# A shared feed-forward's second stage in seven products per unit, added onto rows of x1

## Chip, core, metric

The kernel runs on one core of a Trainium2 chip. The metric is the device time of one execution in microseconds. Everything is float32.

## What is computed

```python
# first layer: modulated linear layer, residual
ys = y * scale
d  = rsqrt(einsum('bi,io->bo', ys*ys, weight*weight) + EPS)
x1 = x + einsum('bsi,io->bso', x * ys[:, None, :], weight) * d[:, None, :]

# second layer on 4096 rows of 512: shared feed-forward, and 8 experts of which 2 per row
shared = silu(xf @ w1) * (xf @ w3) @ w2            # 512 -> 1024 -> 512
h      = gelu(einsum('nc,ech->enh', xf, W1e))
y      = einsum('enh,ehc->enc', h, W2e)
routed = einsum('ne,enc->nc', combine, y)          # combine: the gates of the top 2
out    = x1 + (shared + routed) / 3
```

## The kernel before

The 4096 rows of x1 are 8 blocks of 512 (`NB`, `TB`). After a prologue that makes x1 block by block (features on the partitions, in `big`, and rows in the DRAM tensor `x1_d`), a list of units runs, one after the other: the shared feed-forward of blocks 0 to 5 (`early` = 6), 4 units a block (`HU`); then 32 slots, each 256 rows of one expert, and behind a switch as many further slots as the routing needs (2 in this run: 34 in all); then the shared units of blocks 6 and 7. These last two blocks are called the tail here.

**A shared unit** makes 256 of the 1024 hidden columns for 512 rows. Its first stage already is a scheme of seven products in place of eight for a 2 x 2 block product: `product` (L696) with n from 1 to 7, each for w1 and w3, each of two matmuls of 128x128 by 256 columns. One PSUM half, `chain`, gathers products 1, 6, 5 and 3, and ScalarE (`evict`, L741) copies it out between them; `other` holds 2, 4 and 7, and VectorE adds them on (`add`, L746). `begin` issues products 1 and 2, `rest` (L750) the others, the silu, and the product into `h`. The sums of blocks that such a scheme needs are made beforehand on VectorE, `token_sums` for x1 and `weight_sums` for w1 and w3.

**Its second stage** is `second(m)` (L789), plain: for one of the unit's two 128-column pieces of h, four matmuls (one per 128 rows) with all 512 columns of w2. They gather in four PSUM banks over the whole block, `py`. It is issued by the *next* unit's `rest`, in two places (behind product 5 and behind the product into h), so that h is ready. At a block's end L808 adds a third of each bank onto the rows of x1, which `fetch_row` has brought; blocks 0 to 5 store the sum in DRAM as `base_d` (from ScalarE's queue, L810), the tail writes the output (L812).

**A slot** (`Slot`) works the same way, with its second stage in four parts (`part0` to `part3`), issued by the next slot. Its expert's weights, W1e and W2e, take two tiles of `big` (`expert`, L817): slot j takes pair j mod 3. `fetch_first` and `fetch_second` bring them over SP's queue; in the steady state three slots ahead. Its rows are gathered by GpSimd, its result goes to `ys_d` in two stores.

**In the tail** each unit calls `pump` four times, 32 times in all. A pump adds picks (`add_picks`, L1004: for a tile of 128 rows the two experts' rows, times their gates, onto the held row tile) and starts gathers for others (`gather_picks`, L987: fetch the tile's row sum, two indirect transfers from `ys_d` into one of ten places in `big`). Tile i of 32 is gathered in pump 25i/32 rounded down, and added six pumps later.

The order of all engines is written out by hand: each engine runs its instructions as the program issues them. `tasks` (L1046 to L1075) names what else is issued at two points of each unit's `rest`: task 2n and 2n+1 belong to unit n. In a list of tasks, `6 * HU` is task 24, hence unit 12, the first of block 3.

Of the kernel before, what the change touches and what calls it, by code (L numbers as in the profile page):

```python
# [32 lines left out]
P = 128  # L33
# [11 lines left out]
def kernel(  # L45
# [458 lines left out]
    def row_tile(name):  # L504
        return later["row"].tile([P, D], FP, tag="row", name=name)

    def open_pools():
        lin_ctx.close()
        later["row"] = ctx.enter_context(tc.tile_pool(name="row", bufs=15))
        work = ctx.enter_context(tc.tile_pool(name="work", bufs=1))  # L510
        t_tiles.append(work.tile([P, 3 * KH * TH], FP, name="t1"))
        later["g"] = work.tile([P, 2 * TB], FP, name="g")
        later["h"] = [work.tile([P, 2 * TB], FP, name=f"h{i}") for i in range(2)]
        rt = rt_ctx.enter_context(tc.tile_pool(name="rt", bufs=1))
        for name in ("sel", "hit", "one", "two"):
            later[name] = rt.tile([P, NT, E], FP, name=name)
        for name in ("picked", "run"):
            later[name] = rt.tile([P, E, NT], FP, name=name)
        for name in ("top", "den", "live", "half"):
            later[name] = rt.tile([P, NT], FP, name=name)  # L520
        for name in ("cnt", "shift", "ns", "upto"):
            later[name] = rt.tile([P, E], FP, name=name)
        later["last"] = rt.tile([P, E + 1], FP, name="last")
        later["full"] = rt.tile([P, E, N // GS], FP, name="full")
        later["edge"] = rt.tile([P, N // GS], FP, name="edge")
        later["own"] = rt.tile([P, NSLOT, E], FP, name="own")
        later["ownf"] = rt.tile([P, NSLOT], FP, name="ownf")
        later["high"] = [rt.tile([P, NT], I32, name=f"high{i}") for i in range(2)]
        later["low"] = [rt.tile([P, NT], I32, name=f"low{i}") for i in range(2)]
        later["addr"] = addr  # L530
        later["toks_raw"] = toks_raw
# [138 lines left out]
    def pump():  # L670

        if not passed:
            return
        for work in pumps.get(passed[0], []):
            work()
        passed[0] += 1

    held = {}

    def fetch_row(t, rows_d):  # L680
        held[t] = row_tile(f"row{t}")
        nc.sync.dma_start(out=held[t], in_=rows_d[ts(t, P)])

    class Shared:
# [62 lines left out]
        def rest(self, prev, task):  # L750
            g, h = self.c = [t.rearrange("p (m t) -> p m t", m=2) for t in (later["g"], later["h"][self.at % 2])]
            self.h = h
            self.evict(0, LO)
            for i in range(2):
                self.product(self.chain[i][:, LO], i, 6, False)
                if not self.seven:
                    self.product(self.other[i][:, HI], i, 7, True)
            self.add(LO, 0, LO)
            pump()
            self.evict(1, LO)  # L760
            for i in range(2):
                self.product(self.chain[i][:, LO], i, 5, False)
            self.evict(1, HI)
            if prev is not None:
                prev.second(0)
            self.add(HI, 1, HI)
            pump()
            for i in range(2):
                self.product(self.chain[i][:, LO], i, 3, False)
            nc.scalar.activation(g[:, 0, HI], self.chain[0][:, LO], AF.Silu)  # L770
            nc.scalar.activation(g[:, 0, LO], g[:, 0, LO], AF.Silu)
            nc.vector.tensor_tensor(h[:, 0, HI], g[:, 0, HI], self.chain[1][:, LO], ALU.mult)  # L772
            nc.vector.tensor_tensor(h[:, 0, LO], g[:, 0, LO], h[:, 0, LO], ALU.mult)
            task(2 * self.at)
            pump()
            if prev is not None:
                prev.second(1)
            for i in range(2):
                self.product(self.other[i][:, HI], i, 4, False)
            self.add(HI, 1, LO)  # L780
            nc.scalar.activation(g[:, 1, :], g[:, 1, :], AF.Silu)
            nc.vector.tensor_tensor(h[:, 1, :], g[:, 1, :], h[:, 1, :], ALU.mult)
            task(2 * self.at + 1)
            pump()

        def parts(self):
            return [lambda: self.second(0), lambda: None, lambda: self.second(1), lambda: None]

        def second(self, m):  # L789
# [12 lines left out]
            if blk < early and HSC - 1 > hc >= HSC - 1 - NS:  # L802
                fetch_row(blk * NS + hc - (HSC - 1 - NS), x1_d)
            if hc == HSC - 1:
                for s in range(NS):
                    t = blk * NS + s
                    r = held.pop(t)
                    nc.vector.scalar_tensor_tensor(r, self.py[blk][s], third, r, ALU.mult, ALU.add)  # L808
                    if blk < early:
                        nc.scalar.dma_start(out=base_d[ts(t, P)], in_=r)  # L810
                    else:
                        nc.sync.dma_start(out=out_f[ts(t, P)], in_=r)  # L812
# [4 lines left out]
    def expert(j):  # L817
        weights[j] = (big[j % PAIRS * 2], big[j % PAIRS * 2 + 1])
# [39 lines left out]
    class Slot:  # L858
# [26 lines left out]
        def rest(self, prev, task):  # L885
            parts = prev.parts()
# [61 lines left out]
        def parts(self):  # L948
            return [self.part0, self.part1, self.part2, self.part3]

        def part0(self):
            j = self.j
            self.r = [row_tile(f"yr{j}_{s}") for s in range(SUB)]
# [17 lines left out]
        def part3(self):  # L971
# [5 lines left out]
            for s in range(SUB):  # L977
                nc.scalar.dma_start(out=ys_d[ds(j * GS + s * P, P)], in_=self.r[s])
# [8 lines left out]
    def gather_picks(t):  # L987

        fetch_row(t, base_d if t < early * NS else x1_d)
        spot = len(order) % 10 * 2  # L990
# [13 lines left out]
    def add_picks(t):  # L1004
        for i, y in enumerate(picks.pop(t)):
            nc.vector.scalar_tensor_tensor(held[t], y, gate[i][:, t : t + 1], held[t], ALU.mult, ALU.add)  # L1006
        if t < early * NS:
            nc.sync.dma_start(out=out_f[ts(t, P)], in_=held.pop(t))
# [14 lines left out]

    def turn_last():
        x1T[last_blk] = big[0]
        for k in range(KC):
            nc.vector.transpose(big[0][:, k, :], later["segs"][:, : TB // Q, ts(k, Q)])

# [17 lines left out]
    for u, work in (  # L1046
# [6 lines left out]
        (6 * HU, [lambda: fetch_weights(0)]),  # L1053
# [3 lines left out]
        (8 * HU + 2, [lambda: fetch_weights(1)]),  # L1057
        (10 * HU + 4, [lambda: turn_rows(0)]),
        (2 * early * HU, [lambda: fetch_weights(2)]),
        (2 * late, [reload_last]),  # L1060
# [13 lines left out]
    for blk in range(1, early):  # L1074
        tasks[2 * blk * HU - 3].append(lambda blk=blk: token_sums(blk))  # L1075
    mine = list(range(early * NS))
    mine = [early * NS + i for i in range(NS)] + mine[: len(mine) // 2] + list(range(NT - NS, NT)) + mine[len(mine) // 2 :]
    points = 4 * TAIL * HU
    for i, t in enumerate(mine):
        p = i * (points - 7) // len(mine)  # L1080
        pumps.setdefault(p, []).append(lambda t=t: gather_picks(t))
        pumps.setdefault(p + 6, []).insert(0, lambda t=t: add_picks(t))
# [10 lines left out]
    for u, unit in enumerate(units):  # L1093
        if u == late:
            for n in tc.Switch(later["spare"], E):
# [8 lines left out]
                for part in last.parts():  # L1104
                    part()
# [3 lines left out]
        if u == late:  # L1109
            passed.append(0)  # L1110
            token_sums(early)
# [3 lines left out]
    prev.second(0)  # L1115
    prev.second(1)
# [39 lines left out]
```

## Time and profile before

| | |
|---|---|
| runs shown, us | 1220.57, 1212.42, 1218.62 (median 1218.62) |
| profiled execution | 1208.25 us, span 1206.5 us, mean granted TensorE clock 0.997 |
| busy, share of the span | TensorE 99%, VectorE 46%, ScalarE 19%, GpSimd 37% |
| prologue (to the first unit's second stage) | 0 to about 160 us |
| blocks 0 to 5 | to about 591 us |
| slots | about 591 to 1048 us |
| tail | about 1048 to 1206.5 us |
| shared unit, TensorE | 18.95 us, of which the second stage 6.87 |

PE is TensorE's matmuls, PEld its weight loads, DVE VectorE, ACT ScalarE, POOL GpSimd, SP the engine that issues most transfers. In the tables of groups a row has the line, engine, operation, output and inputs, shape and count; then busy time and the mean duration of one in ns; then how long its engine sat idle before it. In timelines a row begins with its start and the time it covers, both in us. A program's float32 matmul is two records. A matmul's duration includes a stretch in which the next one is already running, so what it costs is the distance to the next one's start. The same holds, less strongly, for VectorE.

### The profile page before, as it was taken

The numbers are of one execution on the slowest core, as the hardware profiler recorded it, in microseconds if no ns is written. First come the engines' busy times: TensorE is split into PE (matmuls) and PEld (weight loads), VectorE is DVE, ScalarE is ACT, GpSimd is POOL, SyncE is SP. The second block draws the span as 40 slices with busy tenths as digits, with TensorE's granted clock in tenths as the row PEclk, the third lists the DMA queues.
The fourth block names the chain that finished last, engine by engine and source line by source line (L and its number), as shares of the span: only waits on it lengthen the run. The fifth ranks groups of instructions, "written<-read, shape, count | busy, mean of one in ns | idle before, by whom it ended". The sixth has DMA issues, their size and how long they took to land.

```text
span 1206.5 us, 14504 instructions
## 1 busy us (share of the span) xinstructions
PE 1189.7 (99%) x4802; PEld 895.5 (74%) x4802; DVE 552.6 (46%) x1264; ACT 225.6 (19%) x515; POOL 449.4 (37%) x448
## 2 busy tenths in 40 slices
PE   9999999999999999999999999999999998999998
PEld 6444666777767677676688888888888887777765
DVE  4546465422323223332255455455455453447664
ACT  2000121211112112121121221221221221121111
POOL 3000000343530112101456676676676670066540
PEclk9999999999999999999999999999999998999999
DMA  9598503201103032110198898999899996287862
GB/s 173 111 230 187 105 27 104 46 0 36 36 1 110 24 133 87 36 70 5 34 253 261 228 236 242 252 238 246 246 238 245 252 241 193 83 258 251 309 227 79
DMA packets 121587, 184.91 MB, mean 153 GB/s; under 512 B 15236, under 2 KB 50180, under 8 KB 121496
## 3 DMA queue, kind: packets, MB, share of 16 engines
q1 hardware_dynamic: 83384, 117.63, 38.0%
q0 software_dynamic: 16448, 35.26, 10.3%
q10 hardware_dynamic: 21664, 30.94, 8.1%
q8 instruction: 40, 0.66, 0.3%
q14 instruction: 51, 0.42, 0.2%
HBM read 139.14 MB, written 44.64 MB: 152 GB/s over the span
## 4 chain that ended last, share of the span: by engine, by line
PE 94%; DMA 4%; DVE 1%; issue 1%; SPq 0%; ACTq 0%; ACT 0%; DVEq 0%
PE ph L875 19%; PE ch L717 18%; PE ps L795 18%; PE ot L717 14%; PE yc L933 9%; PE pl L443 8%; PE yo L933 7%; DMA big<-in_L_cond_W1e_dram 2%; DMA seg<-in_x_dram 1%; PE pq L372 1%; DMA ys_d<-yr 1%; DMA w0t<-in_L_cond_weight_dram 0%; PE pr L388 0%; DVE xT L282 0%; DVE row L1006 0%
## 5 line engine op out<-in xcount | busy, mean ns | idle before, releaser
L844 POOL DMA_INDIRECT xsegs<-x_d,toks x280 | 307.1, 1097 | 327.4 <-issue 127.7
L795 PE MATMUL ps<-w_sb,h 128*128 128x512 f32 x512 | 230.0, 592 | 0.0
L648 POOL DMA_INDIRECT tok_d<-token,addr x64 | 63.5, 992 | 289.7 <-DVE addr L638 275.1
L795 PEld LDWEIGHTS ps<-w_sb,h 128*128 128x128 f32 x512 | 97.3, 190 | 95.6 <-issue 92.1
L875 PE MATMUL ph<-xg,big 128*128 128x256 f32 x544 | 130.3, 383 | 5.0 <-issue 4.3
L946 DVE TENSOR_TENSOR yr<-yo,yr 128x256 f32<-128x256 f32 x102 | 43.3, 424 | 191.0 <-ACT yr L943 95.3
L875 PE MATMUL ph<-t,big 128*128 128x256 f32 x544 | 128.5, 379 | 0.0
L875 PEld LDWEIGHTS ph<-xg,big 128*128 128x128 f32 x544 | 104.3, 192 | 21.0 <-issue 5.6
L443 PE MATMUL pl<-xT,wm 128*128 128x512 f32 (+1 forms) x288 | 117.0, 554 | 0.8 <-DVE big L354 0.4
L748 DVE TENSOR_TENSOR g<-ot,g 128x256 f32<-128x256 f32 x96 | 40.6, 423 | 161.9 <-PE ot L717 139.1
L875 PEld LDWEIGHTS ph<-t,big 128*128 128x128 f32 x544 | 103.4, 190 | 14.1
L717 PE MATMUL ot<-big,w_sb 128*128 128x256 f32 x448 | 110.3, 379 | 0.0
L996 POOL DMA_INDIRECT big<-ys_d,addr x64 | 69.3, 1082 | 101.5 <-PE ch L717 58.6
L717 PEld LDWEIGHTS ot<-big,w_sb 128*128 128x128 f32 x448 | 85.0, 190 | 12.4 <-issue 0.8
L443 PEld LDWEIGHTS pl<-xT,wm 128*128 128x128 f32 x288 | 52.4, 190 | 52.1 <-issue 46.5
L943 ACT ACTIVATE yr<-yc 128x256 f32<-128x256 f32 x136 | 52.3, 384 | 204.7 <-PE yc L933 194.4
L933 PE MATMUL yc<-w0t,g 128*128 128x256 f32 x272 | 69.9, 379 | 0.5 <-ACT yr L943 0.5
L883 ACT ACTIVATE h<-ph 128x512 f32<-128x512 f32 x68 | 40.6, 598 | 157.6 <-PE ph L875 157.6
L748 DVE TENSOR_TENSOR h<-ot,h 128x256 f32<-128x256 f32 x96 | 40.6, 423 | 60.3 <-PE ot L717 48.7
L772 DVE TENSOR_TENSOR h<-g,ch 128x256 f32<-128x256 f32 x32 | 13.5, 421 | 118.1 <-PE ch L717 115.6
L717 PE MATMUL ch<-w0t,seg 128*128 128x256 f32 x256 | 62.6, 380 | 2.5 <-issue 2.5
L717 PE MATMUL ch<-t,seg 128*128 128x256 f32 x256 | 63.1, 379 | 0.0
(184 smaller groups left out, 1454.4 us busy)
## 6 DMA issues: line engine op xcount, KB each, us to landing
big<-in_L_cond_W1e_dram SPq DMA_DIRECT2D x140, 256.0 KB, 6.2
big<-in_L_cond_W2e_dram SPq DMA_DIRECT2D x34, 1024.0 KB, 6.4
ys_d<-yr ACTq DMA_DIRECT2D x68, 256.0 KB, 5.5
x_d<-back SPq DMA_DIRECT2D x32, 256.0 KB, 4.8
row<-x_d SPq DMA_DIRECT2D x32, 256.0 KB, 4.6
out_dram<-row SPq DMA_DIRECT2D x32, 256.0 KB, 4.0
base_d<-row ACTq DMA_DIRECT2D x24, 256.0 KB, 4.2
row<-base_d SPq DMA_DIRECT2D x24, 256.0 KB, 4.9
```

Of the source, the lines that this page charges most:

```text
L443: nc.tensor.matmul(pas[oc][:, ds(lo, n)], lhsT=wms[b][:, k, oc, :], rhs=xTs[blk][:, k, ds(lo, n)], start=(k == 0), stop=(k == KC - 1),)
L648: ins = nc.gpsimd.indirect_dma_start(out=tok_d, out_offset=bass.IndirectOffsetOnAxis(ap=later["addr"][i][:, t : t + 1].bitcast(U32), axis= ...
L717: nc.tensor.matmul(out, lhsT=lhs[:, k, :], rhs=rhs[:, k, :], start=start and k == 0, stop=k == KH - 1, skip_group_check=not start,)
L748: nc.vector.tensor_tensor(c[:, m, cols], p[:, half], c[:, m, cols], ALU.add)
L795: nc.tensor.matmul(self.py[blk][s], lhsT=self.h[:, m, ts(s, P)], rhs=w2_sb[:, hc, :], start=(hc == 0), stop=(hc == HSC - 1),)
L844: nc.gpsimd.indirect_dma_start(out=seg[:, q, :], out_offset=None, in_=x1_segs, in_offset=bass.IndirectOffsetOnAxis(ap=toks[:, c : c + 1].b ...
L875: nc.tensor.matmul(self.ph[:, i], lhsT=weights[j][0][:, k, ts(c, P)], rhs=xg[j][:, k, :], start=(k == 0), stop=(k == KC - 1),)
L883: nc.scalar.activation(self.h[:, ds(c - i, per), :], self.ph, AF.Gelu)
L933: nc.tensor.matmul(out, lhsT=a[:, k, :], rhs=b[:, k, :], start=start and k == 0, stop=k == HC // 2 - 1, skip_group_check=not start,)
L943: nc.scalar.activation(self.r[r][:, cols], self.chain[:, LO], AF.Copy)
L946: nc.vector.tensor_tensor(self.r[r][:, cols], self.other[:, half], self.r[r][:, cols], ALU.add)
L996: nc.gpsimd.indirect_dma_start(out=picks[t][i], out_offset=None, in_=ys_d, in_offset=bass.IndirectOffsetOnAxis(ap=at.bitcast(U32), axis=0) ...
```

## The change

In blocks 1 to 7 the second stage becomes the 7-product scheme, over the unit's 256 hidden columns and 512 rows. h is taken as 2 x 2 blocks (`a11` to `a22`: rows 0 to 255 or 256 to 511, first or second 128 hidden columns), and so is the unit's part of w2. Block 0 keeps the plain form (`plain`).

- `hidden_sums`: 4 VectorE sums at a unit's end make s1, s2, s4 and, in place, a21.
- `out_sums`: 3 VectorE sums per unit of a block, t1, t2 and t4, in block 1 (held in `big[0]`) and once more for the tail (`big[5]`); in block 1 also one in place in w2.
- `seconds(part)`: 14 matmuls of 256 columns in four parts, into three banks: `chain` takes four products, `two` one, `seven` two.
- `drain(part)`: 7 VectorE operations add a third of a bank onto the base rows at once, unit by unit; `chain` is drained after each of its products and filled again. So the block's sums no longer gather in PSUM.
- The base rows are fetched at a block's start, in tiles of two 128-row tiles (`pair_tile`, 6 of them in place of 15 row tiles), and stored by SP. Rows fetched for the tail use GpSimd's segment buffer too. Sums, outputs and `ys_d` also move in pairs.
- The tiles of `big` are dealt to the slots in another way, and weights are fetched at other tasks; picks have eight places in `big[1]` to `big[4]`.
- In the tail, tiles 0 to 19 are picked before block 7's, 20 to 23 after it.

```diff
-    held = {}
-    def fetch_row(t, rows_d):
-        held[t] = row_tile(f"row{t}")
-        nc.sync.dma_start(out=held[t], in_=rows_d[ts(t, P)])
+    def fetch_pairs(blk, tiles=None):
+        base[blk] = tiles or [pair_tile(f"base{blk}_{m}") for m in range(2)]
+        for m, r in enumerate(base[blk]):
+            nc.sync.dma_start(out=r, in_=as_pair(x1_d, blk * TB + m * TH))
+    def out_sums(u, home):
+        tiles = [home.rearrange("p k (n d) -> p (k n) d", d=TH)[:, n] for n in range(8)] + later["more"]
+        t1, t2, t4 = out_map[u] = tiles[3 * u : 3 * u + 3]
+        b1, b2 = w2_sb[:, 2 * u, :], w2_sb[:, 2 * u + 1, :]
+        b11, b12, b21, b22 = b1[:, LO], b1[:, HI], b2[:, LO], b2[:, HI]
+        if u not in summed:
+            nc.vector.tensor_tensor(b12, b22, b12, ALU.subtract)
+            summed.add(u)
+        nc.vector.tensor_tensor(t2, b12, b11, ALU.add)
+        nc.vector.tensor_tensor(t1, b22, t2, ALU.subtract)
+        nc.vector.tensor_tensor(t4, b21, t2, ALU.subtract)
...
             self.evict(1, LO)
+            mm, drain = parts[0]
+            mm()
+            drain()
             for i in range(2):
                 self.product(self.chain[i][:, LO], i, 5, False)
             self.evict(1, HI)
-            if prev is not None:
-                prev.second(0)
+            mm, drain = parts[1]
+            mm()
             self.add(HI, 1, HI)
+            drain()
             pump()
             for i in range(2):
                 self.product(self.chain[i][:, LO], i, 3, False)
...
+            mm, drain = parts[2]
+            mm()
             nc.vector.tensor_tensor(h[:, 0, HI], g[:, 0, HI], self.chain[1][:, LO], ALU.mult)
             nc.vector.tensor_tensor(h[:, 0, LO], g[:, 0, LO], h[:, 0, LO], ALU.mult)
+            drain()
             task(2 * self.at)
             pump()
-            if prev is not None:
-                prev.second(1)
             for i in range(2):
                 self.product(self.other[i][:, HI], i, 4, False)
+            mm, drain = parts[3]
+            mm()
             self.add(HI, 1, LO)
             nc.scalar.activation(g[:, 1, :], g[:, 1, :], AF.Silu)
+            drain()
             nc.vector.tensor_tensor(h[:, 1, :], g[:, 1, :], h[:, 1, :], ALU.mult)
+            if self.blk > 0:
+                self.hidden_sums()
             task(2 * self.at + 1)
             pump()
+        def hidden_sums(self):
+            s1, s2, s4 = later["hs"]
+            nc.vector.tensor_tensor(s1, a21, a22, ALU.add)
+            nc.vector.tensor_tensor(s2, s1, a11, ALU.subtract)
+            nc.vector.tensor_tensor(a21, a11, a21, ALU.subtract)
+            nc.vector.tensor_tensor(s4, a12, s2, ALU.subtract)
+        def seconds(self, part):
...
+            for out, a, b, start in (
+                [(chain, a11, b1[:, LO], True), (two, a12, b2[:, LO], True)],
+                [(seven, a21, b1[:, HI], True), (chain, s2, t2, False)],
+                [(chain, s1, t1, False)],
+                [(chain, s4, b2[:, HI], False), (seven, a22, t4, False)],
+            )[part]:
+                for s in range(2):
+                    nc.tensor.matmul(out[:, s], lhsT=a[:, ts(s, P)], rhs=b, ...)
+        def drain(self, part):
+            for bank, m, half in (
+                [(chain, 0, LO), (two, 0, LO)],
+                [(seven, 1, HI), (chain, 1, LO)],
+                [(chain, 1, HI)],
+                [(chain, 0, HI), (seven, 1, LO)],
+            )[part]:
+                r = base[blk][m][:, :, half]
+                nc.vector.scalar_tensor_tensor(r, bank, third, r, ALU.mult, ALU.add)
+            if part == 3 and self.u == HU - 1:
+                self.store()
...
-        weights[j] = (big[j % PAIRS * 2], big[j % PAIRS * 2 + 1])
+        weights[j] = ((big[2], big[3]), (big[4], big[5]), (big[1], big[0]))[j % PAIRS]
...
-            for s in range(SUB):
-                nc.scalar.dma_start(out=ys_d[ds(j * GS + s * P, P)], in_=self.r[s])
+            nc.scalar.dma_start(out=as_pair(ys_d, j * GS), in_=self.pair)
...
-        spot = len(order) % 10 * 2
+        spot = len(order) % 8 * 2
...
-        (6 * HU, [lambda: fetch_weights(0)]),
+        (8 * HU + 1, [lambda: fetch_weights(0)]),
-        (8 * HU + 2, [lambda: fetch_weights(1)]),
+        (10 * HU + 1, [lambda: fetch_first(1)]),
+        (10 * HU + 4, [lambda: fetch_first(2)]),
         (10 * HU + 4, [lambda: turn_rows(0)]),
-        (2 * early * HU, [lambda: fetch_weights(2)]),
-        (2 * late, [reload_last]),
+        (2 * early * HU, [lambda: fetch_second(1), lambda: fetch_second(2)]),
+        (2 * late, [reload_last, lambda: out_sums(0, big[5])]),
+        (2 * late + 1, [lambda: out_sums(1, big[5])]),
+        (2 * late + 3, [lambda: out_sums(2, big[5])]),
...
+    for blk in range(early):
+        tasks[2 * blk * HU].append(lambda blk=blk: fetch_pairs(blk))
+    for u in range(HU):
+        tasks[2 * HU + 2 * u].append(lambda u=u: out_sums(u, big[0]))
...
-    prev.second(0)
-    prev.second(1)
+    for mm, drain in prev.parts():
+        mm()
+        drain()
```

## The prediction, made blind

> **What bounds the kernel now.** I read the page's busy table first, then the chain of waits, the costliest groups, and last the timelines of the places that the change touches. The page:
>
> ```profile
> PE 1189.7 (99%) x4802; PEld 895.5 (74%) x4802; DVE 552.6 (46%) x1264; ACT 225.6 (19%) x515; POOL 449.4 (37%) x448
> ...
> PE 94%; DMA 4%; DVE 1%; issue 1%; SPq 0%; ACTq 0%; ACT 0%; DVEq 0%
> PE ph L875 19%; PE ch L717 18%; PE ps L795 18%; PE ot L717 14%; PE yc L933 9%; PE pl L443 8%; PE yo L933 7%; DMA big<-in_L_cond_W1e_dram 2%; DMA seg<-in_x_dram 1%; PE pq L372 1%; DMA ys_d<-yr 1%; DMA w0t<-in_L_cond_weight_dram 0%; PE pr L388 0%; DVE xT L282 0%; DVE row L1006 0%
> ...
> L795 PE MATMUL ps<-w_sb,h 128*128 128x512 f32 x512 | 230.0, 592 | 0.0
> ```
>
> TensorE is busy 99% of the span and 94% of the chain. L795, which the change replaces in seven blocks of eight, is 18% of the chain and never waits (idle 0.0). So PE time saved there is span saved, as long as nothing else comes late.
>
> What does a matmul cost? Its duration (592 ns) overlaps its neighbours', so I take distances between starts, from the PE timeline of a quiet block:
>
> ```profile
> 239.43 3.60 PE L795 MATMUL ps<-w_sb,h 128*128 128x512 f32 x8
> 242.86 1.89 PE L717 MATMUL ch<-big,seg 128*128 128x256 f32 x8
> 244.59 3.60 PE L795 MATMUL ps<-w_sb,h 128*128 128x512 f32 x8
> ```
>
> A program matmul is two records. Eight records of 512 columns take 242.86 - 239.43 = 3.43 us, so one matmul 0.858; eight of 256 columns take 1.73, so one 0.432. Halving the width costs nothing extra: the 190 ns weight load fits behind each 216 ns record.
>
> **What it saves.** Old: a unit's second stage is 2 x 4 matmuls of 512 columns, 6.87 us. New: 7 products of 2 matmuls of 256 columns, 14 x 0.432 = 6.04. Saved 0.82 a unit, in 7 x 4 = 28 units: **23.1 us**. A full unit becomes 12.09 (first stage, 28 x 0.432) + 6.04 = 18.1 us, from 18.95.
>
> **What it adds on VectorE.** Per unit 7 drains of a whole bank (L808's form: 128x512, one PSUM input, result added to SBUF) and 4 hidden sums (128x256); per block it removes 4 L808. The nearest rows, from the VectorE timelines of a tail unit and of block 0:
>
> ```profile
> 1091.50 2.98 DVE L1006 SCALAR_TENSOR_TENSOR row<-big,gate,row 128x512 f32<-128x512 f32 x4
> 1094.39 0.21 DVE L995 COPY addr<-idx 128x1 int32<-128x1 int32 x2
> ...
> 1135.97 2.47 DVE L808 SCALAR_TENSOR_TENSOR row<-ps,row 128x512 f32<-128x512 f32 x4
> ...
> 170.06 0.42 DVE L424 TENSOR_TENSOR seg<-w_sb 128x256 f32<-128x256 f32 x1
> 170.51 0.42 DVE L425 TENSOR_TENSOR seg<-seg,w_sb 128x256 f32<-128x256 f32 x1
> ```
>
> Back to back a drain costs 0.60 ((2.47 - 0.69)/3), four sums of the hidden kind 1.46 (L424 to the next add at 171.52). So 7 x 0.60 + 1.46 = 5.7 us more a unit.
>
> In blocks 1 to 5 VectorE works 4 to 7 of 19 us, so capacity is free; what can bite is order. The chain bank is filled, drained, filled again: a link PE -> drain -> PE costs 0.2 (L808 starts 0.17 after PE) + 0.69 + 0.07 (yc waits 0.47 for an ACT copy of 0.38, which leaves 0.09) = 0.96. Between parts 0 and 1 stand p5 and the `seven` product, between 1 and 2 p3, between 2 and 3 p4: at least 1.73 us of other PE work. Cover left: 0.76 a link, so cost **0**; without cover up to 0.96 each. The first-stage adds behind a drain in VectorE's queue have over 3 us before PE needs their bank. The w2 sums (4 ops, 1.5 us, four times in block 1) fall behind block 0's last 4 L808 in one unit: 0.2.
>
> **The tail (blocks 6, 7).** There VectorE also adds the picks. A tail unit held this:
>
> ```profile
> 1100.00:1119.00 19.00, 19.00 (x74) 13.71 (x73) 13.94 (x34) 3.62 (x9) 10.94 (x11) 1.00 0.88 297
> 1119.00:1138.00 19.00, 19.00 (x74) 13.71 (x73) 13.52 (x33) 3.62 (x9) 10.92 (x11) 1.00 0.81 269
> ```
>
> (third figure: VectorE, 13.9 of 19 us). By distances between starts a new unit asks 3 pairs of adds 2.0 + products 1.3 + drains 4.2 + sums 1.5 + 5.12 tiles of picks x (2 x 0.72 + 0.12) = 8.0: 17.0 of 18.1 us. It fits, barely. [...]
>
> With 17.0 of 18.1 the order still bites. I laid the queue out unit by unit, with pumps at p = 25i/32. PE waits where a pump of two tiles (2.9 us) stands ahead of a drain in a link: behind the four transposes of turn_last plus a double pump, 1.5 (second tail unit; there was 0.28 before); the double pump ahead of drain 2 in the third unit 1.6 and in the fourth 1.3 (each late by 2.2 against 0.76 cover); 0.3 in the fifth and sixth. Sum about **5.0**; it can be 1 (if picks slip between)[...]. The pick spots go from 10 to 8: a gather then follows the add of eight picks before, in the same pump or the next; its data is used 6 pumps (27 us) later, so 0.
>
> **The end.** Now:
>
> ```profile
> 1195.47 7.03 PE L795 MATMUL ps<-w_sb,h 128*128 128x512 f32 x16
> ...
> 1202.54 0.69 DVE L808 SCALAR_TENSOR_TENSOR row<-ps,row 128x512 f32<-128x512 f32 x1 [0.17 <-PE ps L795]
> ```
>
> After 1203.2 the last store takes 3.3 us to the end. In the new kernel the last unit's four parts stand alone. Counted from the last p4: PE ends part 3 of the unit before at 1.7; `two` waits for the product into h (to 3.4), `seven` for the hidden sums (4.6), the chain for its drain behind them (5.6), then two links uncovered. PE ends 3.2 later than its 6.04 us alone would, VectorE 3.35 later. Then two stores of 512 KB 0.9 us apart in place of four of 256 KB: between +0.3 and +3.3 (a doubled tail); I take 1.5. Together **4.9**.
>
> **Moved steps.** Bytes are as before; issues halve. base_d stores leave ACT's queue (24) for SP's (12): SP waits in part 3 of each block's successor for the drains, and behind it stand the fetches of weights. At slot 0 the order on SP becomes store (1 MB), first half of slot 3, then the *second* halves of slots 1 and 2; slot 2's first half and slot 0's go earlier, into quiet blocks. Slot 2's first matmul waited 0.77 for that transfer: gone. Instead slot 1's W2e is issued some 18 us into slot 0 and lands 6 to 10 later, where weight_sums of slot 1 wants it at 23. VectorE may stand 1 to 6 us, with other_sums queued behind it, but PE needs these sums only at about 29 to 32. Taken: **-0.8**; range -0.8 to +3. x1, sum and ys pairs: six buffers of two rows for fifteen rows; in the tail about five pairs are in flight beside the held base pair, and a late fetch has six pumps of cover: 0 (bound +2).
>
> **Sum.** -23.1 + 0.2 + 5.0 + 4.9 - 0.8 = -13.8 us on the profiled run's 1208.25 (span 1206.5 and 1.75 around it): 1194.5, or 0.9886. On the median 1218.62, itself 0.9% above the profiled run, that is **1205**.
>
> **Rivals.**
> - *VectorE bounds the tail* ([...]every link there late): 8 us more than taken, 1213. For: 17.0 of 18.1 leaves no room. Against: the x4 rows. 0.20.
> - *Little stalls*: tail 1, end 3: 1199. For: the present tail waits once, for 0.28, at a like order of queue. Against: the end's links are plain. 0.20.
> - *The ring is late everywhere (slower)*: in all 28 units drains 1 and 2 miss PE by the full link, 2 x 0.96 - 0.82 = +1.1 each, with the end's 4.9: +36, 1254. It undoes the gain from 0.65 us of wait a unit ((23.1 - 4.9)/28) and is slower by over 1% from 1.1. For it: two links per unit have only 0.76 of cover. Against: it needs VectorE 1.7 us late each time, and blocks 1 to 5 have an idle VectorE there (4.39 us before L772). 0.07.
> - *It doesn't save what it says*: narrower matmuls expose loads. Every 256-column row of L717, L875 and L933 has the 0.432 distance beside its 190 ns load. 0.03, at 1218.
>
> Likeliest case (0.50): 1205, own range 1199 to 1211.
>
> **Numbers.** About 1% (12.2 us) is what a measurement here tells from no change. Range 1195 to 1218: it leaves out the ring case and the ends. The likeliest case lies at 1.1%, so two thirds of it counts as faster, with all of the second rival and a little of the first: 0.33 + 0.20 + 0.03 = 0.56; slower 0.07; the rest 0.37.
>
> **What would show it.** L795 down to 64 records; a new line with 784 records of 128x256 at 0.216 us; a unit of blocks 1 to 5 at 18.1 us with no PE wait on a drain (shows the ring covered); in the tail PE waits on drains of 1 to 1.6 us in the second to fourth unit, VectorE over 16 us a unit; 16.6 us from the last p4's end to the end of the span (now 11.0: 1195.5 to 1206.5); no wait at slot 2. Wrong if PE waits on drains in quiet blocks, if tail units all stretch past 19 us, or if slot 1 or 2 waits for W2e.

## The result, and the profile after

| kernel | us, median (lowest to highest) | profiled execution | span | clock |
|---|---|---|---|---|
| before, 17 timings beside the changed kernel | 1219.35 (1212.42 to 1227.91) | 1208.25 | 1206.5 | 0.997 |
| changed, 17 timings | 1205.09 (1198.46 to 1214.17) | 1203.78 | 1202.0 | 0.995 |

The ratio is 0.9882, with an interval of 0.9853 to 0.9911: 14 us faster, and the median is the forecast's 1205. The two profiled executions tell a different story: between them lie only 4.5 us, where the sum said 13.8. So the total came out right, and by these two profiles the sum did not. What follows is about that gap: most of it turns out to be waits that come and go in any kernel here. The page of the changed kernel:

```profile
PE 1171.5 (97%) x5138; PEld 958.1 (80%) x5138; DVE 710.4 (59%) x1569; ACT 224.7 (19%) x515; POOL 448.5 (37%) x448
...
PE 84%; DVE 6%; DMA 5%; issue 2%; SPq 2%; ACT 0%; ACTq 0%; DVEq 0%
PE ph L970 18%; PE ch L749 16%; PE ot L749 12%; PE yc L1028 9%; PE sa L862 7%; PE yo L1028 7%; PE pl L443 6%; PE sc L862 3%; PE ps L896 2%; DMA seg<-in_x_dram 2%; PE sb L862 2%; DVE sum L1107 1%; DMA big<-in_L_cond_W2e_dram 1%; DVE xsegs L881 1%; DVE base L881 1%
```

TensorE is 18 us less busy, but 84% of the chain instead of 94%: VectorE's drains (L881) and picks (L1107) now stand in it. Of the groups of TensorE's instructions, shapes kept apart, two rows stand for the second stage:

```profile
L862 PE MATMUL sb<-w_sb,h 128*128 128x256 f32 x112 | 28.8, 380 | 0.6 <-DVE h L824 0.6
...
L896 PE MATMUL ps<-w_sb,h 128*128 128x512 f32 x64 | 28.8, 592 | 0.0
```

The plain form is down to block 0's 64 records; `two`'s 112 records are one seventh of the new form's 784.

Where the time went, by the timelines of both profiled executions, with what the prediction's sum put into the same stretch:

| stretch | before | changed | difference | forecast |
|---|---|---|---|---|
| to the first second stage | 160.42 | 161.88 | +1.46 | 0 |
| block 0 | 60.05 | 61.75 | +1.70 | 0 |
| blocks 1 to 5 | 370.43 | 355.12 | -15.31 | -15.4 |
| slots | 457.21 | 458.24 | +1.03 | -1.6 |
| tail | 158.39 | 165.01 | +6.62 | +3.3 |
| span | 1206.5 | 1202.0 | -4.5 | -13.8 |

(Forecast of the blocks: 19 units at 0.823 and the 0.2; of the slots: one unit's 0.82 and the 0.8; of the tail: 8 units' 6.6 less, 5.0 and 4.9 more. Rounding leaves 0.1.) The saving in blocks 1 to 5 came out as forecast; 9.3 us are missing outside. A quiet unit, from the changed kernel's timeline (start, time covered):

```profile
372.41 1.03 PE L862 MATMUL sa<-more,hs 128*128 128x256 f32 x4
372.61 0.69 DVE L881 SCALAR_TENSOR_TENSOR base<-sc,base 128x512 f32<-128x512 f32 x1
373.27 1.89 PE L749 MATMUL ch<-big,seg 128*128 128x256 f32 x8
373.48 0.69 DVE L881 SCALAR_TENSOR_TENSOR base<-sa,base 128x512 f32<-128x512 f32 x1 [0.17 <-PE sa L862]
375.00 1.03 PE L862 MATMUL sa<-more,hs 128*128 128x256 f32 x4
```

The chain bank `sa` is filled from 372.41, drained from 373.48 to 374.17, and filled again at 375.00. Such a step, fill, drain, fill again, is a link, and the other TensorE work inside it is its cover. TensorE doesn't wait: 375.00 - 374.17 = 0.83 is left, less the 0.05 of the handover (in the tail, below, a drain ends at 1092.00 and the product behind it starts at 1092.05). The next unit is 18.13 us on, as forecast.

**The slots.** Slot 1's second weights come late, and here it is TensorE that waits for them:

```profile
598.44 5.91 SPq L924 DMA_DIRECT2D big<-in_L_cond_W2e_dram  x3
604.65 1.89 PE L970 MATMUL ph<-xg,big 128*128 128x256 f32 x8
608.66 0.69 DVE L1016 TENSOR_TENSOR w0t<-big 128x512 f32<-128x512 f32 x1 [6.43 <-DMA big<-in_L_cond_W2e_dram]
608.70 1.10 PE L1028 MATMUL yc<-big,h 128*128 128x256 f32 x4 [2.17 <-DMA big<-in_L_cond_W2e_dram]
```

The first of the three transfers, issued at 598.44, is slot 1's; the other two are for slots 2 and 3. Both engines go on 10.2 us later. The stage adds up by its listed waits: the unit's 0.82 less, slot 2's wait of 0.77 gone, this 2.17 more, and the wait behind the switch, which every profile has, 4.68 instead of 4.26: +1.00, measured +1.03.

**The tail.** First a wait of the second tail unit, then the third tail unit, where `sa` has to be drained ahead of its fourth product:

```profile
1069.85 2.48 DVE L1131 STREAM_TRANSPOSE big<-xsegs 128x512 f32<-128x512 f32 x4
...
1072.25 2.95 DVE L1107 SCALAR_TENSOR_TENSOR xsegs<-big,gate,xsegs 128x512 f32<-128x512 f32 x4
...
1075.71 1.99 PE L749 MATMUL ot<-x1T,w_sb 128*128 128x256 f32 x8 [1.32 <-DVE g L780]
...
1087.62 2.98 DVE L1107 SCALAR_TENSOR_TENSOR sum<-big,gate,sum 128x512 f32<-128x512 f32 x4
...
1087.90 1.03 PE L862 MATMUL sa<-big,hs 128*128 128x256 f32 x4
...
1091.32 0.68 DVE L881 SCALAR_TENSOR_TENSOR base<-sa,base 128x512 f32<-128x512 f32 x1
1091.91 1.52 DVE L1107 SCALAR_TENSOR_TENSOR sum<-big,gate,sum 128x512 f32<-128x512 f32 x2
1092.05 1.13 PE L862 MATMUL sa<-w_sb,hs 128*128 128x256 f32 x4 [1.40 <-DVE base L881]
```

In the third unit the product is done at about 1088.8, but the double pump (four picks) has begun at 1087.62 and the drain comes only at 1091.32. That is the order of queue which the prediction laid out. In the second unit four transposes and a double pump stand in the queue as laid out too, but what TensorE waits for behind them is not a drain: it is the first stage's add (L780), which frees the bank `ot`. The middle of the tail by windows, each a unit (sum and mean rows left out; third figure: VectorE):

```profile
1101.65:1121.28 19.63, 18.40 (x86) 15.88 (x85) 17.95 (x46) 3.62 (x9) 13.11 (x12) 1.00 0.82 271
1121.28:1140.00 18.72, 18.62 (x85) 15.71 (x84) 16.93 (x41) 3.62 (x9) 11.01 (x11) 1.00 0.86 293
1140.00:1158.72 18.72, 18.62 (x85) 15.71 (x84) 18.26 (x43) 3.62 (x9) 9.83 (x10) 1.00 0.81 271
```

The third window holds more VectorE work (18.26 us) than the first (17.95), and yet it takes 0.9 us less. So it isn't VectorE's capacity that stretches a unit to 19.6, but where a drain stands in its queue. The end:

```profile
1188.85 1.10 PE L862 MATMUL sb<-w_sb,h 128*128 128x256 f32 x4 [0.61 <-DVE h L824]
...
1190.11 1.10 PE L862 MATMUL sc<-w_sb,h 128*128 128x256 f32 x4 [0.15 <-DVE h L836]
...
1191.61 0.68 DVE L881 SCALAR_TENSOR_TENSOR xsegs<-sc,xsegs 128x512 f32<-128x512 f32 x1
1192.21 0.68 DVE L881 SCALAR_TENSOR_TENSOR xsegs<-sa,xsegs 128x512 f32<-128x512 f32 x1
1192.94 1.13 PE L862 MATMUL sa<-more,hs 128*128 128x256 f32 x4 [0.86 <-DVE xsegs L881]
...
1194.86 1.13 PE L862 MATMUL sa<-w_sb,hs 128*128 128x256 f32 x4 [0.78 <-DVE xsegs L881]
...
1196.89 0.69 DVE L881 SCALAR_TENSOR_TENSOR xsegs<-sc,xsegs 128x512 f32<-128x512 f32 x1 [0.17 <-PE sc L862]
```

The last parts begin at 1187.21 and TensorE ends at 1196.69: 9.48 us for 6.04 of matmuls. After the last drain (1197.58) the stores take 4.4 us, before 3.3. From the end of the last p4 (product 4 of the first stage; 1185.49) to the end of the span it is 16.5 us; the forecast was 16.6.

### The profile page after: what moved, and what is told of

Read it like the earlier page. It is cut to its first block, busy times and chain, and to the rows that moved or that the text cites. A ratio compares the mean times of both kernels' runs of the same rounds, so it can differ in the third digit from the quotient of the medians.

```text
span 1202.0 us, 15347 instructions
## 1 busy us (share of the span) xinstructions
PE 1171.5 (97%) x5138; PEld 958.1 (80%) x5138; DVE 710.4 (59%) x1569; ACT 224.7 (19%) x515; POOL 448.5 (37%) x448
## 4 chain that ended last, share of the span: by engine, by line
PE 84%; DVE 6%; DMA 5%; issue 2%; SPq 2%; ACT 0%; ACTq 0%; DVEq 0%
PE ph L970 18%; PE ch L749 16%; PE ot L749 12%; PE yc L1028 9%; PE sa L862 7%; PE yo L1028 7%; PE pl L443 6%; PE sc L862 3%; PE ps L896 2%; DMA seg<-in_x_dram 2%; PE sb L862 2%; DVE sum L1107 1%; DMA big<-in_L_cond_W2e_dram 1%; DVE xsegs L881 1%; DVE base L881 1%
## 5 line engine op out<-in xcount | busy, mean ns | idle before, releaser
L780 DVE TENSOR_TENSOR g<-ot,g 128x256 f32<-128x256 f32 x96 | 40.4, 421 | 60.8 <-PE ot L749 30.9
L776 ACT ACTIVATE g<-ch 128x256 f32<-128x256 f32 x96 | 36.7, 382 | 209.6 <-PE ch L749 152.2
L881 DVE SCALAR_TENSOR_TENSOR base<-sa,base 128x512 f32<-128x512 f32 x88 | 60.7, 690 | 19.6 <-PE sa L862 18.5
L780 DVE TENSOR_TENSOR h<-ot,h 128x256 f32<-128x256 f32 x96 | 40.6, 423 | 51.7 <-PE ot L749 36.6
L1028 PEld LDWEIGHTS yc<-w0t,g 128*128 128x128 f32 x272 | 51.4, 190 | 8.2 <-ACT yr L1038 1.3
```

The source lines that it names most:

```text
L780: nc.vector.tensor_tensor(c[:, m, cols], p[:, half], c[:, m, cols], ALU.add)
L881: nc.vector.scalar_tensor_tensor(r, bank, third, r, ALU.mult, ALU.add)
L1028: nc.tensor.matmul(out, lhsT=a[:, k, :], rhs=b[:, k, :], start=start and k == 0, stop=k == HC // 2 - 1, skip_group_check=not start,)
```

## The experiments

The kernels of one set were timed together, beside the kernel before; its level moved between the sets (1219, 1209, 1219), so only ratios are compared, and traces.

| set | kernel | us, median | before | ratio, interval |
|---|---|---|---|---|
| 1 | kernel before, one execution | 1225.89 | 1219.29 | |
| 1 | changed kernel | 1202.37 | 1219.29 | 0.9851, 0.9797 to 0.9905 |
| 1 | plain tail | 1199.21 | 1219.29 | 0.9827, 0.9779 to 0.9875 |
| 1 | earlier W2e | 1201.71 | 1219.29 | 0.9851, 0.9806 to 0.9897 |
| 2 | last block plain | 1194.67 | 1209.16 | 0.9886, 0.9871 to 0.9901 |
| 2 | plain tail and earlier W2e | 1190.09 | 1209.16 | 0.9846, 0.9832 to 0.9860 |
| 2 | no adds of picks, one execution | 1191.93 | 1209.16 | |
| 2 | fewer gathers, one execution | 1199.51 | 1209.16 | |
| 3 | changed kernel | 1203.21 | 1218.56 | 0.9868, 0.9847 to 0.9889 |
| 3 | plain tail and earlier W2e | 1197.63 | 1218.56 | 0.9829, 0.9803 to 0.9856 |
| 3 | drains twice, one execution | 1215.81 | 1218.56 | |
| 3 | drains three times, one execution | 1236.38 | 1218.56 | |

**1. Both kernels again (no edit).**

> The kernel before, unchanged, for a second profile. Its first profiled run took 1208.25 us, less than the fastest of its 17 timed runs (1212.42, median 1219.35). Theory 'a lucky look': stages that the change does not touch (prologue, issue stall in block 0, switch behind slot 31) differ between executions by several us, so a second profile is longer by 4 us or more, and the extra lies in those stages; blocks 1 to 5 stay at 18.95 us a unit. Rival 'outside the span': the stages agree within 1 us with the first profile and timed runs are longer only around the span.

> The changed kernel, unchanged. Theory 'by the program': what its first profile lost against the sum recurs: slot 1 waits some 2 us for its W2e, the tail takes 165 us with the second tail unit at about 21.6, the third at 21.4, the fourth at 19.6. Rival 'by chance': the second tail unit's 1.1 and 1.4 us waits (ScalarE and VectorE idle 3 to 5 us with nothing in the profile to wait for) are gone or elsewhere, and the tail is 162 us or less, as the sum had it. Ratio to before 0.988 by both.

The second profile of the kernel before has a span of 1223.9 instead of 1206.5. Its slots took 463.96 us (457.21 in the first profile) and its tail 166.2 (158.39), with the same instructions; the prologue took 1.2 more and block 0 1.7. Its timeline inside the slots:

```profile
905.29 1.89 PE L875 MATMUL ph<-t,big 128*128 128x256 f32 x8
910.30 1.73 PE L933 MATMUL yc<-big,g 128*128 128x256 f32 x4 [3.12 <-issue]
911.83 1.91 PE L933 MATMUL yo<-w0t,h 128*128 128x256 f32 x4
913.54 2.18 PE L875 MATMUL ph<-xg,big 128*128 128x256 f32 x8
```

TensorE stands for 3.12 us with nothing shown that it waits for ("issue"). After that four records take 1.71 us to the next start (911.83 to 913.54) where they take 0.86 elsewhere: the work behind the wait runs at half speed. The first profile, on which the whole sum was made, has but one such wait in slots and tail, the 4.26 us behind the switch. Its 1208.25 lies below all 17 timings beside the changed kernel (lowest 1212.42): for them it is an unusually quiet execution, though in set 2 it would be an ordinary one (1206.65 to 1210.31). The changed kernel's three profiles lie at 1202.0, 1202.5 and 1210.0; its first is an ordinary one. Its second repeats most of the losses, as the theory "by the program" had it: a wait of 1.24 us on W2e, a tail of 165.6, third and fourth tail units of 19.79 and 19.62. The second tail unit's waits are partly elsewhere.

**2. Where the clock goes.** The windows of the changed kernel's third profile, from its slots (third figure from the right: granted clock):

```profile
888.00:892.00 4.00, 1.53 (x7) 1.37 (x8) 0.26 (x1) 0.38 (x1) 3.07 (x3) 1.00 0.95 215
892.00:896.00 4.00, 1.33 (x7) 0.82 (x5) 0.00 (x0) 0.23 (x1) 3.06 (x3) 0.94 0.72 146
896.00:900.00 4.00, 3.79 (x9) 3.08 (x10) 2.32 (x4) 1.14 (x3) 0.00 (x0) 0.50 0.22 35
900.00:904.00 4.00, 4.00 (x14) 3.28 (x14) 2.20 (x5) 0.15 (x1) 0.00 (x0) 0.71 0.97 321
```

Behind two "issue" waits of 2.9 us the clock is at one half for 6.8 us (twice 0.06 x 4, 0.50 x 4 and 0.29 x 4). It explains block 0's +1.70 as well: a wait of 2.5 us at about 180 us stands in the profiles of both kernels. Where the window behind it shows 0.57 (changed kernel), a stretch from the first second stage to the slots takes 1.69 us more than where it shows 1.00. In the ten profiles with the changed kernel's blocks 1 to 5 that stretch is 415.18 to 415.19 without the drop (five) and 416.86 to 416.88 with it (five). The same wait costs 1.7 us or nothing; the runs show no reason for the one or the other.

**3. The tail plain again, blocks 6 and 7.** The second stage of the tail's blocks goes back to 512-column matmuls, the difference in w2 is undone, and the tail's `out_sums` go.

```diff
+    def plain_again(u):
+        b12, b22 = w2_sb[:, 2 * u, HI], w2_sb[:, 2 * u + 1, HI]
+        nc.vector.tensor_tensor(b12, b22, b12, ALU.subtract)
...
-            if self.blk > 0:
+            if 0 < self.blk < early:
                 self.hidden_sums()
...
-            if self.blk == 0:
+            if self.blk == 0 or self.blk >= early:
...
```

> The change in blocks 1 to 5 alone; blocks 6 and 7 go back to the plain second stage (w2's piece changed in place is restored by 4 sums). Theory 'the tail gives it back': in the profiles the tail went from 158.4 to 165.0 us, so this should bring it back to about 159, 6 us less than the changed kernel: ratio to before about 0.983. Rival 'the tail pays too': if the changed tail's extra waits are chance, undoing it loses the 6.6 us of TensorE work that seven products save in eight units: ratio 0.990 to 0.994.

0.9827 against the changed kernel's 0.9851 in the same set: 3 us less where 6 were expected, and the intervals overlap. The traces say it more sharply. The plain tail took 161.7 us here, beside 165.6 of the changed kernel in the same set; with the kernel of 5, which has the same tail, it took 164.8 beside 166.4 in set 3, and 158.5 in set 2, beside 161.6 of a changed tail there (6 below). It is shorter each time, by 1.7 to 3.9 us. The tail's seven products save 6.6 us of TensorE and give back more.

**4. The second weights of slot 1 one step earlier.**

```diff
-        (2 * early * HU, [lambda: fetch_second(1), lambda: fetch_second(2)]),
+        (2 * early * HU - 1, [lambda: fetch_second(1)]),
+        (2 * early * HU, [lambda: fetch_second(2)]),
```

> The changed kernel, but W2e of slot 1 is fetched one task earlier (behind the last unit of block 5, whose x1 held its place, and ahead of the store of base rows and of slot 3's W1e on SP). Theory 'order on the queue': it lands some 7 us earlier, slot 1's and TensorE's wait of 2.2 us go, ratio 0.986. Rival 'bytes': the transfers of slots 1 to 3 are limited by their bytes (4 MB at some 250 GB/s), the wait only moves to slot 2 or 3, ratio unchanged at 0.988.

The wait on W2e (2.17, 1.24 and 1.32 us in the changed kernel's profiles) is gone from the trace: TensorE's product at 606.72 starts with none, and none has moved to slot 2 or 3. The time shows no difference, 0.9851 and 0.9851; this execution had an "issue" wait of 2.92 us at 865.74 instead. A gain of 2 us is below what these timings resolve.

**5. Only the last block plain, and the two edits of 3 and 4 together.** The first edit is that of 3 with `last_blk` in place of `early`.

```diff
-            if self.blk == 0:
+            if self.blk in (0, last_blk):
...
+        (2 * (late + HU) + 1, [lambda u=u: plain_again(u) for u in range(HU)]),
```

> Block 7 alone goes back to the plain second stage (32 matmuls of 512 columns in 4 units, with the difference added back onto the second weights); block 6 keeps the seven products. Theory (the tail gives back what it saves, and most of that at the end): PE loses 4 x 0.82 = 3.3 us in block 7, but the exposed last unit ends as before the change, 3.4 us earlier relative to its own matmuls, and the stores at the end shrink by 1; the third- and fourth-unit waits behind VectorE stay. So 1 us below the changed kernel, ratio 0.984. Rival (the end costs nothing that matters, saved matmuls are all that counts): 3.3 us above the changed kernel, ratio 0.991.

> Blocks 6 and 7 plain, and slot 1's second weights fetched one step earlier. If the parts add up: the 3 us of the plain tail, and 1 to 2 us of the wait on W2e: ratio 0.981. If the wait on W2e only hides another wait behind it (the run with the earlier fetch alone showed the same 0.985 as the changed kernel): the plain tail's own 0.983.

> Blocks 6 and 7 plain and the earlier fetch of slot 1's second weights. Theory: 5 to 8 us below the changed kernel of the same job. Rival (its lead in the last job was a matter of that job): within 3 us of it.

The last block alone gave 0.9886, between the two expectations of 0.984 and 0.991; the changed kernel wasn't in that set, so the ratio can't decide. By the traces its tail is 160.4 us, 1.3 below the 161.6 of the changed tail in an execution without unexplained waits (6 below), as the theory's 1. Both edits together gave 0.9846 in the same set, higher than both expectations (0.981 and 0.983), and 0.9829 in the other, where the changed kernel had 0.9868: 5.6 us below it, inside the expected 5 to 8, with intervals that just overlap. Of all versions this one has the lowest ratio in both sets that hold it.

**6. What VectorE's queue and the gathers do in the tail.** In one kernel the picks aren't added (one column is, so that the gathers are still waited for), in the other the first twelve tiles aren't gathered.

```diff
-            nc.vector.scalar_tensor_tensor(r, y, gate[i][:, t : t + 1], r, ALU.mult, ALU.add)
+            if i == 0:
+                nc.vector.tensor_tensor(r[:, :1], y[:, :1], r[:, :1], ALU.add)
```

```diff
-            nc.gpsimd.indirect_dma_start(
+            if len(order) > 12:
+              nc.gpsimd.indirect_dma_start(
```

> Leaves out the adding of the picks (146 VectorE adds of 0.74 us in the tail become half as many one-column adds); gathers, matmuls and stores stay. If VectorE's queue sets the tail's waits: the waits of 1.2 to 1.5 us at the third, fourth and fifth tail units vanish (together 4 us less), VectorE falls to about 11 of 18.1 us a unit, and the tail unit is 18.1 us; the end keeps 3 us of waits. The stall in the second tail unit, where ScalarE and VectorE both stand for 3 to 5 us with no wait shown, stays, if it comes from the transfers of the first gathers. If the tail's waits come from elsewhere (transfers, POOL): all stay.

> Leaves out the gathers of the first 12 tiles of picks (24 indirect transfers of 256 KB); their adds read what the buffers held. If ScalarE and VectorE stand in the second tail unit because the transfer queues are full then: both stand less than 1 us there (in the changed kernel 5.3 and 3.5), PE waits under 0.5 in that unit, and the waits of the third and later units stay at 1.2 to 1.5. If it is code of the second unit that comes late whatever the transfers do: the same 3 to 5 us.

Unit lengths in the tail, from the start of each unit's `two` product to the next one's:

| unit | 2nd | 3rd | 4th | 5th | 6th | 7th |
|---|---|---|---|---|---|---|
| changed, first profile | 23.19 | 19.79 | 19.63 | 18.72 | 18.72 | 18.14 |
| changed, third profile | 24.60 | 19.79 | 19.62 | 18.72 | 18.72 | 18.13 |
| fewer gathers | 19.72 | 19.77 | 19.68 | 18.72 | 18.72 | 18.13 |
| no adds of picks | 18.13 | 18.13 | 18.13 | 18.13 | 18.13 | 18.13 |

Without the adds every unit takes 18.13 us, and behind the first one no wait is left but the end's. Two of its units by windows:

```profile
1092.49:1110.62 18.13, 18.13 (x86) 15.96 (x85) 11.12 (x37) 3.62 (x9) 10.81 (x11) 1.00 0.92 313
1110.62:1128.75 18.13, 18.13 (x86) 15.96 (x85) 11.19 (x36) 3.62 (x9) 10.22 (x10) 1.00 0.85 287
```

The transfers and GpSimd are as busy as before, VectorE has 11.1 us. So the picks stretch the tail, 6.0 us in all by the third row (1.59 + 1.64 + 1.55 + 0.59 + 0.59); the tail is 6.1 shorter (155.5 against 161.6). More than the 4 expected: a wait that shows 1.3 stretches its unit by 1.6, and the fifth and sixth units lose 0.6 with no wait listed. Taking the adds away takes both their place in the queue and their load away; that it is the place rests on the windows above. No run moved the picks and kept their number.

The second unit's further 3.5 to 4.9 us are another matter. In the changed kernel's first profile:

```profile
1059.15 0.38 ACT L776 ACTIVATE g<-ch 128x256 f32<-128x256 f32 x1 [5.35 <-PE sa L862]
...
1062.79 0.69 DVE L881 SCALAR_TENSOR_TENSOR xsegs<-sa,xsegs 128x512 f32<-128x512 f32 x1 [1.51 <-PE sc L862]
1063.54 1.13 PE L862 MATMUL sa<-big,hs 128*128 128x256 f32 x4 [1.10 <-DVE xsegs L881]
...
1066.09 1.99 PE L749 MATMUL ch<-x1T,seg 128*128 128x256 f32 x8 [1.42 <-ACT g L776]
```

ScalarE and VectorE stand although what they are said to wait for is long done. With fewer gathers that is gone, which looks like proof that the transfers cause it; but it is gone with all gathers in place too, without the adds of the picks and with the last block plain, all runs of set 2. In sets 1 and 3 it is there in every profile, the kernel before's and the plain tail's included. It goes with the set, not with the edit, and its cause stays open.

**7. The cover of the ring.** In blocks 1 to 5 the chain's drains of parts 1 and 2 are repeated, once in one kernel (`again = 1`) and twice in the other, whose edit this is.

```diff
-                nc.vector.scalar_tensor_tensor(r, bank, third, r, ALU.mult, ALU.add)
+                again = 2 if blk < early and part in (1, 2) and bank is chain else 0
+                for _ in range(1 + again):
+                    nc.vector.scalar_tensor_tensor(r, bank, third, r, ALU.mult, ALU.add)
```

> In blocks 1 to 5 the drains of the chain in parts 1 and 2 are each done twice (so those products count twice in the output): each link is 0.60 us longer. With a cover of 0.76 a link, as the prediction has it: no PE wait on L881 in these blocks, a unit of 18.13 us, time as the changed kernel's. If the cover is thinner: 0.1 to 0.6 per link, 4 to 24 us in all.

> The same drains done three times: each link is 1.2 us longer. With a cover of 0.76: PE waits 0.44 at each of two links a unit, in 20 units, 17 us in all, and a unit takes 19.0 us. If VectorE's drains don't hold PE at all: 18.13. If the whole addition shows: 2.4 a unit, 48 us.

Done twice, no wait recurs (one of 0.18 in the first unit), and the unit takes 18.23 instead of 18.13. The whole, 1215.81, was expected at the changed kernel's time (1203.21) and is 12.6 above it; 10 us of the excess against the changed kernel's first profile lie in the slots, which the edit doesn't touch (468.2 us instead of 458.2, with 4.1 on W2e and several unexplained waits). Done three times:

```profile
383.20 1.03 PE L862 MATMUL sa<-more,hs 128*128 128x256 f32 x4
...
384.27 2.14 DVE L883 SCALAR_TENSOR_TENSOR base<-sa,base 128x512 f32<-128x512 f32 x3 [0.17 <-PE sa L862]
...
386.46 1.13 PE L862 MATMUL sa<-more,hs 128*128 128x256 f32 x4 [0.51 <-DVE base L883]
...
389.82 1.13 PE L862 MATMUL sa<-w_sb,hs 128*128 128x256 f32 x4 [0.51 <-DVE base L883]
```

From one chain product to the next it is now 3.26 and 3.36 us instead of 2.59, and the wait recurs in every unit: 19.68 us a unit, 31 us over 20 units. The three drains take 2.14, 1.45 more than one; the link loses 0.67 to 0.77 of that. So the cover is 1.45 less about 0.7, that is 0.7 to 0.8 us. The expected 17 us was too little, since repeated drains of one target cost 0.725 each, not 0.60.

**8. The changed kernel a third time.**

> The changed kernel again, to stand beside the plain-tail kernel in one job. Ledger theory: against a kernel before without unexplained 'issue' waits (1206 to 1210 us) it saves 23.1 in the second stage and gives back about 8 in the tail's waits and end, 1.5 in the slots and 1 to 2 before the first unit: ratio 0.990 to 0.992. If 'issue' waits return in the kernel before (1215 to 1226), the ratio is 0.985 to 0.988. Rival (the saving itself is that of the medians): 0.988 either way.

0.9868 beside a kernel before at 1218.56: in the range expected for that level. The rival, 0.988 at any level, would need the changed kernel timed in a set like 2; no run has that. Two figures of set 2 stand in for it. The one execution with fewer gathers gives 1199.51 to 1209.16: 0.992. An estimate from four timings, those of the last block plain (1194.67) with the 1.3 us added by which its tail is shorter, gives 1195.9: 0.989. They don't agree, and the intervals measured for the changed kernel in the other sets all hold 0.988. The rival stays open.

## Why the prediction was right in total, point by point

- **Saving, 23.1 (0.82 a unit): right.** 18.13 us a unit, 15.31 us in blocks 1 to 5. No part of 256-column work cost extra.
- **The ring covered, 0.76 a link: right.** No wait on a drain in the quiet blocks, and the repeated drains measured 0.7 to 0.8. That closes the slower rival: its price is real (1.55 us a unit once two drains are 1.45 late each), its condition isn't met.
- **Tail waits, "about 5.0": right in place, nearly in size.** Second to sixth unit stretch by 1.6, 1.6, 1.5, 0.6, 0.6, sum 6.0, where the prediction had 1.5, 1.6, 1.3, 0.3, 0.3. Behind turn_last with a double pump, then behind double pumps ahead of drain 2, as laid out; only that in the second unit the late VectorE work was a first-stage add, where the prediction had drains alone in mind. Taking the adds away removed all of it.
- **A drain's 0.60: right where the target changes.** Drains of different targets start 0.60 apart in the tail (1191.61 and 1192.21 at the end of the span) and take 0.68 each, VectorE has 16.9 to 18.3 us a unit, and of the two units with 18.72 us one held more work than the one with 19.63. So the rival that VectorE bounds the tail is out; its 8 us were the author's estimate. Where drains write the same target one after the other, though, they came 0.725 apart ((2.14 - 0.69)/2), no closer than their durations.
- **The end, 4.9: a little too high.** TensorE is 3.4 later (3.2 forecast) and the stores take 1.1 more (1.5). 16.5 us from the last p4, 16.6 forecast. With 6.0 in the tail and this the rival of little stalls is out.
- **The tail's sum** of +3.3 fits an execution without unexplained stalls: 161.6 us with fewer gathers (whose unit lengths from the third on are the changed kernel's within 0.05) against 158.4 before, +3.2. The profiled +6.6 has 3.5 more in the second unit, which no step named.
- **Moved steps, -0.8: the step that failed.** Slot 2's wait did go. But "VectorE may stand 1 to 6 us, but PE needs these sums only at about 29 to 32" overlooked that TensorE itself reads W2e: the product into `yc` at 608.70 takes a piece of the weights straight. VectorE stood for 6.43 us, TensorE for 2.17. The term is about +1.4, inside its stated range (up to +3). Issuing the transfer one step earlier removed the wait.
- **Untouched code, 0: off by 3.2 in the profiled pair.** 1.70 of it is the clock's drop behind a wait that both kernels have; the 1.46 of the prologue comes from waits on VectorE's transposes and residual adds (L282, L354), 0.8 us in the first profile before and 1.1 to 3.2 in all others.
- **"13.8 of the profiled run" put on the median: it held, in part by luck.** Of the 9.3 us that the pair of profiles lacks, 6.6 are waits that came and went in kernels of both kinds: 1.46 in the prologue, 1.70 by the clock, 3.5 in the second tail unit. Most of the rest is what the sum itself had wrong, the W2e wait of 2.17. An estimate for set 2, where the unexplained waits are absent, fits: 1195.9 (8 above) against 1209.16 is 13.2 us; the one execution with fewer gathers gives only 9.7. But the step from one quiet profile to the median of ordinary executions was an assumption: the kernel before lies 10.2 us higher there than in set 2, the changed kernel 9.2 by that estimate, and nothing in the prediction said that both would lose alike. In sets 1 and 3 they did not: there the change saved 16.9 and 15.4 us. Why was not settled.

## What to carry to other kernels

When a scheme trades TensorE work for VectorE drains, count the drain's place in VectorE's queue, not VectorE's load: a unit with 18.3 us of VectorE work took 18.7, one with 18.0 took 19.6. Such a scheme belongs where VectorE is idle; in the tail, where picks share the queue, and in the last unit, where nothing covers the links, the plain form was as fast or faster (the plain tail shorter by 1.7 to 3.9 us, with the last block alone plain by 1.3). For a transfer that is moved, look for every reader, TensorE's direct ones too; and before scaling a sum to a median, see whether the profile's own time lies inside the timings at all.

## What the runs showed of the hardware

- **A wait can cost twice.** Behind waits of 2.5 to 5.2 us the granted clock was often one half, for 3.4 us (0.57 over a window of 4 us) or 6.8; with the drains done twice also for 3.4 us behind one of 1.42 in the second tail unit (0.75 and 0.82 over 1076 to 1080 and 1080 to 1084). In the changed kernel's first profile TensorE stands from 177.54 to 180.06, and the clock is 0.50 from 180.5 to 183.5 and 1.00 from 184 on. In the same profile it is 0.50 from 1000 to 1006, behind the 4.68 us of the wait at the switch; in the first profile of the kernel before, 0.50 from 1012 to 1016, behind its 4.26. The shorter drop cost 1.7 us, and it followed the same wait of 2.5 us in some executions (five of the ten compared in 2) and not in others. Why was not shown.
- **Stalls with no shown cause.** In the second tail unit ScalarE and VectorE stood with nothing shown to wait for (5.35 and 3.48 us in the changed kernel's first profile) in every profile of two sets of runs and in none of a third, for all kernels alike (with the seven products the unit took 3.5 to 5.1 us longer); "issue" waits of 1.7 to 3.3 us in the slots stood in some profiles of those two sets and in none of the third. Small transfers of instructions fall into the stall (two in the second tail unit, of 0.02 and 0.01 MB, between 1057 and 1061), but also into the same place of runs without it (the last block plain, between 1052 and 1055), so they don't explain it.
- **A wait's figure is not its cost.** A listed wait of 0.51 on a drain lengthened its link by 0.67 to 0.77.
